# A gated cross-attention layer on one core: the statistics of pass 1 pinned behind the norms, and two gate projections kept for the passage

## The chip, the core and the metric

The kernel runs on one core of a Trainium2 chip. The core has a matrix engine (PE, TensorE, with PEld as its weight loads), a vector engine (DVE), a scalar engine (ACT), GpSimd (POOL), and SP, which here only issues DMAs. Each engine works through its own queue of instructions in order, and engines wait for one another through semaphores. The metric is the time in microseconds of one execution on the device. Before the change it is 2236.16 us, the median of three runs (2235.13 to 2239.27).

## The reference

All in float32. x is 64 sequences of 128 tokens with 512 features; the context is of the same shape; there are 4 heads of 128. Two residual layers follow one another:

```python
Q, K, V = (per head) LN(x) @ Wh, ctx @ Wh, ctx @ Wh
scores = einsum('bshe,bthe->bhst', Q, K) / sqrt(hd)
masked = scores * Dn[None]
A = maximum(abs(masked.sum(axis=0)), 1.0)     # summed over ALL 64 sequences
O = einsum('hst,bthe->bshe', A, V)
Y = (O - mu) / sqrt(var + 0.001) * gn_gamma + gn_beta
W = relu(LN(x) @ wg_w)
x = x + tanh(g_xattn) * ((W * Y) @ wo_w)
# then, on the new x:
g = (LN(x) @ gate_w.T) * gate_s;  u = (LN(x) @ up_w.T) * up_s
x = x + tanh(g_ffn) * (((silu(g) * u) @ down_w.T) * down_s)
```

The sum over the batch axis is what shapes the kernel: A needs the scores of every sequence before the first output token can be made. So there is a pass over all of x for the scores, and a second pass for everything that uses A.

## The kernel before

**Tiling.** The 64 sequences are 16 groups (NG) of 4 (GB), a group being 512 tokens. A group's x lies in two tiles `x_t` (pool `xin`, five buffers). Large matrix products are done by a seven-product scheme on 2x2 blocks; one `product` (L288) is four matmuls of 128x256, and the trace counts two records for each of them.

**Pass 1** (the loop over g at L592 and after) has, per turn, three generators that `interleave` mixes by their number of steps:
- `prepare(g)`: the statistics of group g on DVE (`bn_stats` L252, `bn_aggr` L253 four times, then `ve` L247) and a power on POOL (L248) that gives `rstd`; then, four times, a norm on DVE (`xn` L280, noted in `last_norm`), four transposes on PE (`pt` L259) and a copy of the result into `xnT` (odd ones on DVE, L514, even ones on ACT, L516).
- `scores(g-1)`: `pq` (L524) from `xnT`, its copy `qw` on ACT, `sv` (L539) with the context tiles, its copy `both` on ACT (L547), a store of the values to DRAM (`v_scr`, L549) by SP, and the running sum `attn` on DVE (L555).
- `project(g-1)`: the gate projection, seven steps of one `product` each (L567 to L588) over four DVE sums `t` (L325), with additions on DVE (`w`, L579 and L582) and copies on ACT; the result is stored to `w_scr`.

The two FFN matrices are rewritten for the seven-product scheme during pass 1 as well: `prepare_weights`, one step per turn, loads a block (SP), sums it on POOL (L325 to L336, L439) and stores it (SP). The parts are wo, five blocks of gate and up weights (`gu_raw`), and three of down weights (`dn_raw`, with ten further sums in a tile `dn_t` that has one buffer). The step's instructions are issued after the turn's x load has been.

**The order on an engine** is decided at build time by a planner which places instructions by its own estimate of when they can start; what the program says with `tc.issue_after(ins)` holds an instruction behind `ins` on its engine. Before, only the statistics of group 1 are held so, behind the last norm of group 0. In the order as built, DVE has the statistics of a group two turns ahead of its norms.

**The passage.** In the last turn (g = 15) the projection of group 14 is given 3 of its 7 steps; what is left of it, and all of the projection of group 15, form `tail`. After the last `sv`, attn is multiplied by the decay, and its absolute value and maximum are taken (L625 to L628). Then two strings spell out the order by hand: T is one step of `tail`, R one of `retention(0)` (`po` L653, its statistics, the transposes `pt` L683, the gated product `w_t`), A one of `attended(0)` (`bx`, `by`, `bz` L731: the output projection, whose weights `wo_w` SP loads, L728; then the norm for the FFN and its transposes), P one of the first four of `retention(1)`.

**Pass 2** runs the FFN of group g (`ffn`: gate and up products at L288, the sums `h` at L336, down products at L1009), interleaved with the rest of the attention of later groups. For g = 0 these are the remaining steps of retention 1, `attended(1)` by way of `late_attended`, and retention 2. In `retention`, WAIT (8) empty steps stand between the loads that turn o into `yT` and the use of it (`yT` scaled on ACT, L703; `w_t` on POOL and DVE, L712); for group 1 there are 3 more. `n_steps` tells `interleave` how many steps the second chain has.

Of the kernel before, what the change touches and what calls it, by code (L numbers as in the profile page):

```python
# [99 lines left out]
def interleave(*weighted):  # L100

    runs = [[gen, steps, 0] for gen, steps in weighted if gen is not None]
    while runs:
        run = min(runs, key=lambda r: (r[2] + 1) / r[1])
        try:
            next(run[0])
            run[2] += 1
        except StopIteration:
            runs.remove(run)


def in_order(steps, **gens):

    for name in steps:
        next(gens[name], None)
    for gen in gens.values():
        for _ in gen:
            pass
# [8 lines left out]
def flamingo_gated_layer(  # L127
# [22 lines left out]
    P = 128  # L150
# [6 lines left out]
    NG = B // GB  # L157
# [36 lines left out]
    def load_ctx(g):  # L194
        tiles = []
        for j in range(GB):
            t = cin.tile([P, H, S], F32, tag="c", name="c_t")
            nc.sync.dma_start(out=t, in_=ctxT[g * GB + j])
            tiles.append(t)
        return tiles  # L200
# [175 lines left out]
    def gate_weights():  # L376

        combine_a(
            nc.gpsimd, [wgc[:, m] for m in (GS1, GS2, GS3, GS4)],
            wgc[:, GA11], wgc[:, GA12], wgc[:, 7], wgc[:, GA22],  # L380
        )
# [116 lines left out]
    def prepare(g, x_t, xnT):  # L498

        n = GB if g else 1  # L500
        for j in range(GB):
            bn(mean_var[:, g * GB + j, :], x_t[j // 2][:, j % 2, :])
            if (j + 1) % n == 0:
                cols = slice(g * GB + j + 1 - n, g * GB + j + 1)
                inv_std(rstd[:, cols], mean_var[:, cols, 1], LN_EPS, n)
        yield
        for j in range(GB):
            b = g * GB + j
            xn = normalised(
                x_t[j // 2][:, j % 2, :], mean_var[:, b, 0:1], rstd[:, b : b + 1]  # L510
            )
            pt = transposed(xn, "pt")
            if j % 2:
                nc.vector.tensor_copy(xnT[:, :, j * S : (j + 1) * S], pt)  # L514
            else:
                nc.scalar.copy(xnT[:, :, j * S : (j + 1) * S], pt)  # L516
            yield
# [73 lines left out]
    pending = None  # L591
    weights = prepare_weights()  # L592
    for g in range(NG):
        x_t, c_t = x_next.pop(0), c_next
        xnT = wide.tile([P, NC, TOK], F32, tag="xT", name="xnT")
        prep = prepare(g, x_t, xnT)
        if g == 1:
            with tc.issue_after(last_norm[0].ins):
                next(prep)
        else:  # L600
            next(prep)
        if g == 1:
            gate_weights()
            constants()
        elif g > 1:
            with tc.issue_after(last_load[0].ins):
                next(weights, None)
        held = project(pending[0], pending[2]) if pending else None

        steps = 3 if g == NG - 1 else 7  # L610
        interleave(
            (prep, GB),
            (scores(*pending) if pending else None, 2 + H),
            (islice(held, steps) if pending else None, steps),
        )
        x_next.append(load_x((g + 2) % NG))
        if g + 1 < NG:
            c_next = load_ctx(g + 1)
        pending = (g, c_t, xnT)
# [26 lines left out]
    def retention(g, v, ws):  # L646

        helper = nc.vector if g < 3 else nc.gpsimd

        o = att.tile([P, GB, H, P], F32, tag="yT", name="o")  # L650
        for h in range(H):
            po = ps_mm.tile([P, GB, P], F32, tag="mm", name="po")
            nc.tensor.matmul(  # L653
                po, lhsT=attn[:, h, :], rhs=v[:, h, :, :], start=True, stop=True
            )
            if g < 2 and h % 2:
                nc.vector.tensor_copy(o[:, :, h, :], po)
            else:
                nc.scalar.copy(o[:, :, h, :], po)
            yield  # L660
        if g:
            sq = att.tile([P, NQ, NC, GB, SQ], F32, tag="sq", name="sq")
        ons = []
        for j in range(GB):
            oj = o[:, j].rearrange("p h e -> p (h e)")
            mv = stat.tile([P, 2], F32, tag="mv", name="mv")
            bn(mv, oj)
            rs = stat.tile([P, 1], F32, tag="rs", name="rs")
            inv_std(rs, mv[:, 1:2], GN_EPS, 1)
            if g:  # L670
                square_transposed(sq, j, normalised(oj, mv[:, 0:1], rs))
            else:
                nc.vector.tensor_scalar(oj, oj, mv[:, 0:1], rs, ALU.subtract, ALU.mult)
                ons.append(oj)
        if g == 0:
            for q in range(2):
                tok = slice(q * HT, (q + 1) * HT)
                for d in range(2):
                    pt = ps_mm.tile([P, KC, HT], F32, tag="mm", name="pt")
                    for c in range(KC):  # L680
                        e = (d * KC + c) * P
                        for i in range(2):
                            nc.tensor.transpose(  # L683
                                pt[:, c, i * P : (i + 1) * P], ons[2 * q + i][:, e : e + P], ident
                            )
                    y = att.tile([P, KC, HT], F32, tag="xn", name="y", bufs=2)
                    for c in range(KC):
                        e = d * KC + c
                        nc.scalar.activation(
                            y[:, c, :], pt[:, c, :], AF.Identity,  # L690
                            scale=gamma_sb[:, e : e + 1], bias=beta_sb[:, e : e + 1],
                        )
                    (helper if d else nc.gpsimd).tensor_tensor(
                        ws[q][:, d], ws[q][:, d], y, ALU.mult
                    )
                    yield
            return
        yT = att.tile([P, NQ, NC, GB, SQ], F32, tag="yT", name="yT")
        moved(yT, sq, sq_scr[0][g % 2])
        for _ in range(WAIT + 3 * (g == 1)):  # L700
            yield
        for e in range(NC):
            nc.scalar.activation(  # L703
                yT[:, :, e], yT[:, :, e], AF.Identity,
                scale=gamma_sb[:, e : e + 1], bias=beta_sb[:, e : e + 1],
            )
        yield
        for d in range(2):
            for q in range(2):
                for k in range(KC):  # L710
                    w = ws[q][:, d, k, :].rearrange("p (g i b) -> p i g b", i=NQ, b=SQ)
                    (helper if d else nc.gpsimd).tensor_tensor(  # L712
                        w, w, yT[:, :, d * KC + k, q * 2 : q * 2 + 2, :], ALU.mult
                    )
            yield
# [82 lines left out]
    WAIT = 8  # L798
    RET_STEPS = 4 + WAIT + 2
    ATT_STEPS = 8 + GB  # L800

    def new_x1nT():
        return wide.tile([P, NQ, NC, GB, SQ], F32, tag="xT", name="x1nT")

    ws = None
# [10 lines left out]
    x_t = x_next.pop(0)  # L816
    first, second = next_retention(0), next_retention(1)
    x1nT = new_x1nT()
    tail = chain(held, project(pending[0], pending[2]))
    for name in "TTRRRRTTTRTRTRTRR":  # L820
        next(tail if name == "T" else first, None)
    in_order("ATATATAAAAAPAPAPAPA", A=attended(0, x_t, ws, x1nT), T=tail, P=islice(second, 4))
    pass1.close()

    AHEAD = 9
# [229 lines left out]
    gu_next = [gate_up(0)]  # L1055
    FFN_STEPS = 2 + 7 * NJ + 3 + (len(DOWN_STEPS) - DOWN_ROOTS + 1) // 2
    def late_attended(g, x_t, x1nT):
        yield from attended(g, x_t, ws, x1nT)

    pending = (0, x_t, x1nT, combine_tokens(nc.vector, x1nT))  # L1060
    for g in range(NG - 1):
        x_t = x_next.pop(0)
        x1nT = new_x1nT()
        if g + 2 < NG:
            x_next.append(load_x(g + 2))
        steps = [attended(g + 1, x_t, ws, x1nT)] if g else [second]
        n_steps = ATT_STEPS + RET_STEPS
        if g == 0:
            steps.append(late_attended(1, x_t, x1nT))
            n_steps += RET_STEPS - 4 + 3  # L1070
        if g + 2 < NG:
            steps.append(next_retention(g + 2))
        interleave(
            (ffn(*pending), FFN_STEPS), (chain(*steps), int(n_steps * 1.4)),
        )
        with tc.issue_after(mid_down[0].ins):
            tokens = combine_tokens(nc.vector, x1nT)
        pending = (g + 1, x_t, x1nT, tokens)
# [59 lines left out]
```

## Time and profile before

| | us |
|---|---|
| median of three runs (range) | 2236.16 (2235.13 to 2239.27) |
| the profiled execution: its own time | 2241.91 |
| the profiled execution: its span | 2240.1 |
| PE busy | 2214.0 (99%) |
| DVE busy | 1171.2 (52%) |
| POOL busy | 666.2 (30%) |
| ACT busy | 640.7 (29%) |
| last `sv` of pass 1 ends, about | 390.4 |
| first product of pass 2 (`bank_a` L891) | 433.95 |

The profile is one execution. Its span is what the engines show from the first to the last instruction; the execution's own time is a little longer. "Busy" is the time in which an engine has an instruction at work, "idle before" the time an engine stood still just ahead of one, with the instruction or DMA that released it. In rows of a timeline, the first number is the start in microseconds from the span's start, the second the duration of the row, `x8` the number of like instructions in it, and the bracket the idle time before. The waits are sums over the span or over a stretch of it: total, count, longest. In a table of windows each engine has its busy time and number of instructions, and the three numbers at the end are the granted clock of PE (1.00 is full speed), the share of time of the DMA engines, and GB/s.

### The profile page before, as it was taken

To read this page: it belongs to the slowest core of one execution; us is meant where nothing else is said; L and a number is where in the kernel's file an instruction comes from. 1 tells how busy PE (TensorE), PEld (TensorE's weight loads), DVE (VectorE), ACT (ScalarE), POOL (GpSimd) and SP (SyncE) were. 2 spreads that over 40 slices of the span, in tenths; PEclk is the share of its full clock that TensorE was granted. 3 is DMA by queue.
4 is the path that set the end of the run, shared out by engine and by line. 5 is a ranking of instruction groups with operands and counts; after the bars stand their busy time and mean duration, and the time that the engine had idled before them with its cause. 6 is when DMAs were issued, how large, how long until landed. Compare 5 with 4: busy or idle time off the path is not lost.

```text
span 2240.1 us, 28797 instructions
## 1 busy us (share of the span) xinstructions
PE 2214.0 (99%) x10112; PEld 1889.5 (84%) x10112; DVE 1171.2 (52%) x2827; ACT 640.7 (29%) x1240; POOL 666.2 (30%) x1047
## 2 busy tenths in 40 slices
PE   8999999999999999999999999999999999999999
PEld 7777788778888888888888888888888888888888
DVE  6445443656464636464646464646464646464524
ACT  3444445322222222222222222222222313131221
POOL 4126300241333333333333332323232424141220
PEclk9999999999999999999999999999999999999999
DMA  9778665667877787777777777777777777766654
GB/s 307 261 271 303 240 231 197 253 221 260 276 255 262 249 267 248 265 247 258 251 263 248 253 255 261 249 266 245 266 244 267 244 271 240 277 214 239 226 181 146
DMA packets 216865, 558.47 MB, mean 249 GB/s; under 512 B 21265, under 2 KB 62993, under 8 KB 199953
## 3 DMA queue, kind: packets, MB, share of 16 engines
q1 hardware_dynamic: 211296, 539.58, 71.8%
q10 hardware_dynamic: 5424, 17.04, 2.0%
q8 instruction: 81, 1.33, 0.2%
q14 instruction: 64, 0.52, 0.1%
HBM read 454.31 MB, written 102.24 MB: 248 GB/s over the span
## 4 chain that ended last, share of the span: by engine, by line
PE 93%; DMA 3%; DVE 2%; POOL 1%; SPq 1%; issue 0%; ACT 0%; ACTq 0%; POOLq 0%; DVEq 0%
PE bank_c L288 21%; PE bank_a L288 14%; PE bank_c L1009 9%; PE bank_f L288 7%; PE bank_b L288 7%; PE bank_b L1009 6%; PE sv L539 4%; PE bank_f L1009 4%; PE bank_a L1009 4%; PE by L731 3%; PE bz L731 2%; PE bx L731 2%; PE po L653 2%; PE pq L524 2%; PE bank_c L891 2%; DMA x_t<-in_x_dram 2%
## 5 line engine op out<-in xcount | busy, mean ns | idle before, releaser
L288 PE MATMUL bank_c<-tcomb,gu 128*128 128x256 f32 x1920 | 454.9, 380 | 1.0 <-DVE c L968 0.7
L288 PEld LDWEIGHTS bank_c<-tcomb,gu 128*128 128x128 f32 x1920 | 363.3, 190 | 59.6 <-issue 6.7
L336 POOL TENSOR_TENSOR h<-h 128x128 f32<-128x128 f32 x576 | 258.6, 481 | 399.3 <-DVE h L881 286.1
L288 PE MATMUL bank_a<-x1nT,gu 128*128 128x256 f32 x1280 | 303.7, 379 | 1.6 <-ACT sil L906 1.6
L288 PEld LDWEIGHTS bank_a<-x1nT,gu 128*128 128x128 f32 x1280 | 242.7, 190 | 47.9 <-issue 13.4
L1009 PE MATMUL bank_c<-dn_w,h 128*128 128x256 f32 x896 | 211.7, 379 | 0.0
L1009 PEld LDWEIGHTS bank_c<-dn_w,h 128*128 128x128 f32 x896 | 170.2, 190 | 23.1
L880 ACT ACTIVATE sil<-c,gs_sb 128x256 f32<-128x256 f32 x176 | 89.3, 508 | 328.9 <-DVE c L968 170.7
L248 POOL TENSOR_TENSOR rs<-ve,mhalf 128x1 f32<-128x1 f32 x128 | 73.5, 586 | 321.7 <-DVE ve L247 221.5
L712 POOL TENSOR_TENSOR w_t<-w_t,yT 128x256 f32<-128x256 f32 x112 | 91.5, 848 | 243.3 <-ACT yT L703 243.3
L742 POOL TENSOR_TENSOR x_t<-x_t,m 128x512 f32<-128x512 f32 x48 | 62.1, 1323 | 341.9 <-ACT m L752 341.9
L968 DVE TENSOR_TENSOR c<-bank_c,m 128x512 f32<-128x512 f32 x80 | 55.3, 691 | 202.4 <-PE bank_c L288 201.0
L1009 PE MATMUL bank_b<-dn_w,h 128*128 128x256 f32 x640 | 156.4, 379 | 0.0
L336 DVE TENSOR_TENSOR h<-h 128x128 f32<-128x128 f32 x608 | 152.5, 308 | 4.3
L288 PE MATMUL bank_f<-tcomb,gu 128*128 128x256 f32 x640 | 151.2, 379 | 0.0
L288 PE MATMUL bank_b<-x1nT,gu 128*128 128x256 f32 x640 | 151.2, 379 | 0.0
L288 PEld LDWEIGHTS bank_b<-x1nT,gu 128*128 128x128 f32 x640 | 121.6, 190 | 22.1 <-issue 6.2
L252 DVE BATCH_NORM_STATS2 st<-x_t 128x6 f32<-128x512 f32 x128 | 83.8, 681 | 103.5 <-DMA x_t<-in_x_dram 102.3
L1009 PEld LDWEIGHTS bank_b<-dn_w,h 128*128 128x128 f32 x640 | 121.6, 190 | 16.5
L288 PEld LDWEIGHTS bank_f<-tcomb,gu 128*128 128x128 f32 x640 | 121.6, 190 | 16.5
L1029 DVE TENSOR_TENSOR x_t<-x_t,bank_c 128x256 f32<-128x256 f32 x192 | 77.6, 419 | 87.7 <-PE bank_c L1009 87.7
L539 PE MATMUL sv<-qw,c_t 128*128 128x256 f32 x512 | 120.5, 379 | 1.8 <-DVE xnT L514 1.8
(152 smaller groups left out, 3292.2 us busy)
## 6 DMA issues: line engine op xcount, KB each, us to landing
dn_w<-dn_scr SPq DMA_DIRECT2D x320, 384.0 KB, 4.9
gu<-gu_scr SPq DMA_DIRECT2D x80, 1024.0 KB, 7.8
gu<-gu_scr SPq DMA_DIRECT2D x80, 768.0 KB, 6.1
x_t<-in_x_dram SPq DMA_DIRECT2D x62, 512.0 KB, 5.4
sq_scr<-sq SPq DMA_DIRECT2D x30, 1024.0 KB, 4.7
wo_w<-wo_scr SPq DMA_DIRECT2D x112, 256.0 KB, 3.9
dn_w<-dn_scr SPq DMA_DIRECT2D x96, 256.0 KB, 5.0
c_t<-in_ctxT_dram SPq DMA_DIRECT2D x64, 256.0 KB, 5.2
```

Source lines behind the costliest of these rows:

```text
L248: nc.gpsimd.tensor_tensor(dst, ve, mhalf[:, :n], ALU.pow)
L252: nc.vector.bn_stats(st, src)
L288: last_product[0] = nc.tensor.matmul(out, lhsT=w[:, s, k, :], rhs=x_k, start=(start and s == 0 and k == 0), stop=(s == 1 and k == KC - 1), ...
L336: engine.tensor_tensor(slots[to], slots[a], slots[b], ALU.add if sign == "+" else ALU.subtract)
L539: nc.tensor.matmul(sv[:, 0 : 2 + i : 1 + i, :], lhsT=c_t[j][:, h, :], rhs=qw[:, h, j : GB + 1 : GB - j, :], start=(i == 0), stop=(i == 1), ...
L712: (helper if d else nc.gpsimd).tensor_tensor(w, w, yT[:, :, d * KC + k, q * 2 : q * 2 + 2, :], ALU.mult)
L731: nc.tensor.matmul(bank[:, i * HN : (i + 1) * HN], lhsT=lhs[:, k, i * P : (i + 1) * P], rhs=w[:, k, :], start=(start and i == 0 and k == 0 ...
L742: engine.tensor_tensor(dst, dst, src.rearrange("p (b d) -> p b d", b=2), ALU.add)
L880: nc.scalar.activation(sil, gate, AF.Silu, scale=gs_sb[:, i : i + 1])
L968: nc.vector.tensor_add(c22, bank_c, m5)
L1009: last_down[0] = nc.tensor.matmul(places[acc], lhsT=hq[q][:, a, :], rhs=dn[n][:, q, :], start=start, stop=True, skip_group_check=True,)
L1029: add = nc.vector.tensor_tensor(dst, dst, places[acc], ALU.add if sign > 0 else ALU.subtract)
```

## The change

Five places are edited. The statistics of every group but the first are now held behind the last norm of the group before it. In the last turn no step of the projection of group 14 is made (`project(14)` isn't begun there), so all 14 steps of the last two projections are in `tail`, and the two strings have three T more between them. Retention 1 has 8 empty steps, as all others, and `attended(1)` begins with four.

```diff
-        if g == 1:
+        if g:
+
             with tc.issue_after(last_norm[0].ins):
                 next(prep)
         else:
...
-        steps = 3 if g == NG - 1 else 7
+        steps = 0 if g == NG - 1 else 7
         interleave(
             (prep, GB),
             (scores(*pending) if pending else None, 2 + H),
-            (islice(held, steps) if pending else None, steps),
+            (islice(held, steps) if pending and steps else None, steps),
         )
...
-        for _ in range(WAIT + 3 * (g == 1)):
+        for _ in range(WAIT):
             yield
...
-    for name in "TTRRRRTTTRTRTRTRR":
+    for name in "TTTRRRRTTTTRTRTRTRR":
         next(tail if name == "T" else first, None)
-    in_order("ATATATAAAAAPAPAPAPA", A=attended(0, x_t, ws, x1nT), T=tail, P=islice(second, 4))
+    in_order("AATATATATAAAPAPAPAPA", A=attended(0, x_t, ws, x1nT), T=tail, P=islice(second, 4))
...
     def late_attended(g, x_t, x1nT):
+        for _ in range(4):
+            yield
         yield from attended(g, x_t, ws, x1nT)
...
-            n_steps += RET_STEPS - 4 + 3
+            n_steps += RET_STEPS - 4 + 4
```

## The prediction

> **What bounds the kernel now.** I read the page's busy shares first, then the waits of PE, then PE's own rows for every gap over 0.1 us, and then the queues of the engines that the gaps name. The busy shares say almost everything about the size of the stakes:
>
> ```profile
> PE 2214.0 (99%) x10112; PEld 1889.5 (84%) x10112; DVE 1171.2 (52%) x2827; ACT 640.7 (29%) x1240; POOL 666.2 (30%) x1047
> ```
>
> PE is busy 2214.0 of the span's 2240.1 us. Its gaps add up to 22.95 us; 6.5 lie in the first 20 us, which the change leaves alone; from 550 us on there is none. So a change of order can win at most 7.9 us in pass 1 (gaps at 85.45, 139.05, 164.22, 189.63, 193.44, 268.25 and 277.08: 1.51, 0.72, 0.95, 1.39, 0.27, 1.23, 1.83) and some 9.5 us in the passage and the first group behind it. PE's list of waits names their causes:
>
> ```profile
> PE pq L524 <- DVE xnT L514: 3.1, 3, 1.4
> PE bx L731 <- POOL w_t L712: 2.5, 2, 1.5
> PE sv L539 <- DVE xnT L514: 1.8, 1, 1.8
> PE by L731 <- DVE st L252: 1.5, 1, 1.5
> PE bank_c L288 <- DVE w L579: 1.5, 1, 1.5
> ```
>
> Each number is the total, the count and the longest. The DVE copies are late because DVE works in order and stands in front of them, waiting for x. The list of waits for the first 400 us shows it (first row), beside POOL, which mostly waits for DVE's `ve`:
>
> ```profile
> POOL rstd L248 <- DVE ve L247: 154.9, 17, 23.8
> DVE st L252 <- DMA x_t<-in_x_dram: 102.3, 25, 8.2
> ```
>
> One instance from DVE's rows: the first bn_stats of a group two ahead waits 6.44 us for its tile, and the norms and copies of the nearer group come behind it.
>
> ```profile
> 255.57 0.69 DVE L252 BATCH_NORM_STATS2 st<-x_t 128x6 f32<-128x512 f32 x1 [6.44 <-DMA x_t<-in_x_dram]
> ...
> 258.98 0.97 DVE L280 TENSOR_SCALAR xn<-x_t,mean_var,rstd 128x512 f32<-128x512 f32 x1
> 259.87 0.68 DVE L582 TENSOR_TENSOR w<-bank_b,m5p 128x512 f32<-128x512 f32 x1
> 260.47 0.67 DVE L514 COPY xnT<-pt 128x512 f32<-128x512 f32 x1
> ```
>
> **Part 1, the pin.** Call the four norms of group g n0 to n3, its statistics (four bn_stats, four aggregates, one `ve`) S(g), the POOL power r(g). Before, DVE ran S two groups ahead of the norms; the built order of the changed kernel puts S(g+1) directly behind n3(g). Nothing is added or removed: 64 bn_stats move. What goes: the 102.3 us of DVE waits for x, since x of group g+1 landed a group earlier. What comes: S and r now stand in the chain from n3(g) to n0(g+1): four bn_stats at 0.6, aggregates and `ve` about 0.9, the power 1.0: some 4.3, 4.9 with hand-offs. Before, n0(g+1) came 5.8 to 12.7 us after n3(g), so DVE alone would be in time.
>
> POOL works in order too. Its weight sums now come between. Per group I put the built order of POOL on the times of its rows: r(2) to r(7) end before their norms are due; r(8) at 185.4 for a copy needed by 189.45; r(9) at 210 with 3.7 us to spare; r(12) to r(15) are safe. r(11) isn't: before, it ran at 222.79, ahead of the last block of down weights; now it stands behind that block's ten dn_t sums, six scalings and seven further sums. POOL's rows of before for that block:
>
> ```profile
> 247.63 1.01 POOL L248 TENSOR_TENSOR rstd<-ve,mhalf 128x4 f32<-128x4 f32 x1 [23.83 <-DVE ve L247]
> 252.39 5.72 POOL L336 TENSOR_TENSOR dn_t<-dn_raw 128x256 f32<-128x256 f32 x8 [3.75 <-DMA dn_scr<-dn_t]
> 258.06 0.92 POOL L336 TENSOR_TENSOR dn_t<-dn_t,dn_raw 128x256 f32<-128x256 f32 x1
> ...
> 259.62 1.60 POOL L439 TENSOR_TENSOR dn_raw<-dn_raw,minus_ds 128x256 f32<-128x256 f32 x2
> ...
> 265.01 6.86 POOL L336 TENSOR_TENSOR dn_raw<-dn_raw 128x256 f32<-128x256 f32 x8
> ```
>
> The sums can't start before 252.39, when the store of the block before has left dn_t. Ten sums, six scalings and seven sums at 0.72 (the 5.72 of eight) are 16.5 us, the power 1.0: about 269.9; at the rows' rate later on, 0.86 (6.86 of eight), it is 272; 269.1 at 0.68. DVE then owes n0(11) 0.54, w of L582 0.69 and the copy behind them 0.68, so the copy ends at 271.0 to 273.9. PE needs that copy for this:
>
> ```profile
> 264.20 1.88 PE L524 MATMUL pq<-xnT,gram 128*128 128x512 f32 x4
> ```
>
> A stall of 6.8 to 9.7 us takes the place of 7.9 us of gaps (the 1.23 and 1.83 just behind it among them). I take 7.5, near the low end, as DVE stands still then and leaves POOL the 0.72. The granted clock is a further term. After the two idles of 1.05 and 1.47 us at 472 to 476, it fell to half:
>
> ```profile
> 476.00:478.00 2.00, 2.00 (x5) 1.64 (x6) 1.34 (x2) 0.00 (x0) 2.00 (x4) 0.50 0.00 0
> ```
>
> Three matmuls there took 2.7 us and not 1.3, so a longer idle costs 1.4 to 1.7 more; single gaps up to 1.83 left it at 1.00. I take 1.5. Pass 1: -7.9 + 7.5 + 1.5 = +1.1; the ends are -7.9 + 6.8 + 1.4 = +0.3 and -7.9 + 9.7 + 1.7 + 0.8 (a late ACT copy behind it, two thirds of the 1.23) = +4.3.
>
> [...]
>
> **Part 2, products kept for the passage.** Last group: 10 of PE's matmuls (4.32 us at 0.432) move from before the last `sv` to behind it. Their work is unchanged, so only cover counts. Let E be the end of the last sv (390.42 before). PE has 12 matmuls, 5.18 us, and then `po`, which needs v. The load of v was issued at 391.64 and landed at 397.43, E + 7.0, hidden by 8.2 us of products; now E + 5.2 leaves 1.85 idle. One product waits for `t` behind the norms, 0.8 to 1.1. Against that, the gaps 0.40, 0.47 and 0.14 before the pt transposes go, and 1.51 at `by`, which in truth waits for a wo_w load (issued 421.84, landed 426.64) that now goes out ahead of w_t's. The 0.56 and 1.60 (an ACT table load) stay: +1.85 + 0.95 - 1.01 - 1.51 is +0.3; my step-by-step sum of the new order gives +0.4. The bounds are +/- 2.0: nothing idle at v and t below, both at full and by's wait kept above. SP issues the same loads as before in another order; one that goes out late is in these bounds.
>
> **Part 3, the wait of retention 1 and the four extra yields.** PE's first `bx` of group 1 waits for POOL's w_t. POOL, before:
>
> ```profile
> 469.10 3.56 POOL L336 TENSOR_TENSOR h<-h 128x128 f32<-128x128 f32 x8 [6.77 <-DVE h L881]
> 472.61 1.41 POOL L712 TENSOR_TENSOR w_t<-w_t,yT 128x256 f32<-128x256 f32 x2
> ```
>
> Built before, 16 h sums of the FFN stand ahead of that w_t; built now, 27. Eleven more at 0.44 (3.56 / 8) are 4.9 us; at 0.70 in the busiest rows, 7.7. The wait is for the same instructions, only later: w_t ends some 5 us on, while PE got one product's 1.3 us more of cover. So +4.9 - 1.3 = +3.6; PE's second wait at 475.99 shrinks by 0.2: +3.4. Ends: +1.0, if the h are ready enough earlier for POOL to fill its 6.77 us of idleness, to +6.0 (7.7 - 1.3 - 0.4). The half clock is there in both kernels. Later groups keep their order and cover.
>
> **Sum.** 1.1 + 0.4 + 3.4 = +4.9. The profiled execution took 2241.91 (span 2240.1 and 1.8 around it), 5.75 over the median of 2236.16; I add the difference to the median: 2241.1. Own range 2236 (0.3 - 1.6 + 1.0 = -0.3) to 2249 (4.3 + 2.4 + 6.0 = 12.7). A measurement of this kernel tells 0.2%, 4.5 us, from no change: under 2231.7 is faster, over 2240.6 slower.
>
> **Rivals.**
> - *The cover on POOL holds* (faster). If r(11) ends by 262.3 (264.20 less 0.54, 0.69, 0.68), PE never waits there and all 7.9 us of pass 1 are won; that needs dn_t free at 245.5, seven us earlier than its store landed. For it: DVE's earlier work may draw PE, and with it SP's store issue at 238.76, forward by the 4.8 us of gaps that lie before. Against: PE's need comes forward as much. With +0.4 and attended(1) at +1: 2229.7. Chance 0.24.
> - *Given back exactly.* Stall at 6.8, v lands before PE asks (-1.6), POOL fills its idleness (+1.0): 0.3 - 1.6 + 1.0, so 2235.9. For it: the terms are of one size and opposed. Chance 0.14.
> - *POOL slower than its rows*: at 0.91 a sum, as in its rows at 194 and 202, r(11) ends past 273 and r(8), with 2 us to spare, is late too; every term at its upper end gives 2248.9. Against: with DVE stalled, POOL is alone. Chance 0.16.
> - *My forecast*, 0.46, of which 0.14 ends under 2240.6.
>
> Faster 0.24, same 0.14 + 0.14 = 0.28, slower 0.32 + 0.16 = 0.48. The range from 2229 to 2249 leaves out about 2 in 10.
>
> **What would show it.** In the changed profile: DVE's waits at L252 for x_t near nothing; POOL's rstd of group 11 near 269 and a PE gap of about 7 us at a pq L524 some 260 us in, released by the xnT copy or the norm, with clock under 1.00 behind it; a PE gap of 1 to 2 us at the first po; bx waiting on w_t for 4 us or more near 475 and none at by. The forecast is wrong if that pq has no gap (faster), or if w_t comes no later than before.

## The result, and the profile after

The changed kernel takes 2242.99 us (median of 13 runs, 2241.48 to 2244.47) against 2236.82 for the kernel before (13 runs beside it): a ratio of 1.0025, 95% interval 1.0017 to 1.0032. It is slower, by some 6 us where 4.9 were forecast. The profiled execution of after took 2244.25, with a span of 2242.5. The page's first lines hide the change entirely:

```profile
PE 2216.7 (99%) x10112; PEld 1893.9 (84%) x10112; DVE 1180.3 (53%) x2827; ACT 642.5 (29%) x1240; POOL 663.4 (30%) x1047
```

PE is "busy" 2.7 us more for the same 10112 instructions: the work is the same and parts of it took longer, at the lower clock that the windows below show. PE's list of waits tells more (total, count, longest):

```profile
PE pq L524 <- DVE xnT L514: 6.8, 1, 6.8
...
PE bx L732 <- POOL w_t L713: 4.3, 1, 4.3
...
PE po L654 <- DMA v<-v_scr: 0.8, 1, 0.8
```

The many small waits of pass 1 are gone; one wait of 6.8 us is left, beside 4.3 us at bx (2.5 before). DVE's own waits show that the pin did what it says: for x it waits 5.7 us in all, where it waited 102.3.

```profile
DVE st L252 <- DMA x_t<-in_x_dram: 5.7, 3, 3.8
```

**The wait of 6.8 us.** It is read backwards, engine by engine. PE's rows:

```profile
258.43 1.89 PE L288 MATMUL bank_a<-xnT,wgc 128*128 128x256 f32 x8
267.11 3.78 PE L524 MATMUL pq<-xnT,gram 128*128 128x512 f32 x4 [6.79 <-DVE xnT L514]
270.68 1.06 PE L259 MATMUL pt<-ident,xn 128*128 128x128 f32 x4
```

DVE, whose copy PE waits for, itself stood still for 13.38 us in front of the first norm of group 11; the copy is two instructions behind that norm and doesn't depend on it:

```profile
247.85 0.70 DVE L247 TENSOR_SCALAR ve<-mean_var 128x4 f32<-128x4 f32 x1
...
264.92 0.94 DVE L280 TENSOR_SCALAR xn<-x_t,mean_var,rstd 128x512 f32<-128x512 f32 x1 [13.38 <-POOL rstd L248]
265.78 0.68 DVE L582 TENSOR_TENSOR w<-bank_b,m5p 128x512 f32<-128x512 f32 x1
266.38 0.68 DVE L514 COPY xnT<-pt 128x512 f32<-128x512 f32 x1
```

And POOL, which had what it needed for that rstd (`ve` ends at 248.55), did 23 sums and scalings first:

```profile
247.80 5.89 POOL L336 TENSOR_TENSOR dn_t<-dn_raw 128x256 f32<-128x256 f32 x8 [22.87 <-DMA dn_scr<-dn_t]
...
259.12 4.80 POOL L336 TENSOR_TENSOR dn_raw<-dn_raw 128x256 f32<-128x256 f32 x7
263.88 1.00 POOL L248 TENSOR_TENSOR rstd<-ve,mhalf 128x4 f32<-128x4 f32 x1
```

POOL had stood idle for 22.87 us just before. The power wasn't ready then; it became ready 0.75 us after the sums began, and its own result came 16.3 us after that.

**The price behind the wait.** The four `pq` records behind the stall take 3.78 us, and 1.88 in the kernel before. The windows of two microseconds show why (the number after the five engines is the granted clock):

```profile
262.00:264.00 2.00, 0.00 (x0) 0.00 (x0) 0.00 (x0) 0.00 (x0) 2.00 (x4) 0.69 1.10 341
264.00:266.00 2.00, 0.00 (x0) 0.00 (x0) 1.08 (x2) 0.00 (x0) 1.57 (x2) 0.50 0.99 301
...
270.00:272.00 2.00, 2.00 (x8) 1.29 (x7) 1.33 (x3) 1.26 (x3) 0.00 (x0) 0.50 1.02 397
272.00:274.00 2.00, 2.00 (x9) 1.69 (x8) 0.33 (x1) 0.36 (x1) 0.00 (x0) 0.75 1.06 400
```

A window's mean clock of 0.69 means that 1.24 of its 2 us were at half: the clock fell at about 262.8 and came back at about 273.0. PE resumed at 267.1 and so worked 5.9 us at half speed, a loss of some 2.9 us on top of the 6.8.

**bx of group 1.** POOL's rows again show a short operation behind many sums:

```profile
469.69 8.07 POOL L336 TENSOR_TENSOR h<-h 128x128 f32<-128x128 f32 x19 [6.76 <-DVE h L882]
477.72 1.40 POOL L713 TENSOR_TENSOR w_t<-w_t,yT 128x256 f32<-128x256 f32 x2
```

**What the two given profiles don't agree on.** The spans differ by 2.4 us (2240.1 and 2242.5), the medians by 6.2. The profiled execution of before took 2241.91, 5 us over its median, so its gaps might not be those of a usual execution. That was the first thing to test.

### The profile page after: what moved, and what is told of

It is laid out like the page before. It is cut to its first block, busy times and chain, and to the rows that moved or that the text cites. A ratio compares the mean times of both kernels' runs of the same rounds, so it can differ in the third digit from the quotient of the medians.

```text
span 2242.5 us, 28798 instructions
## 1 busy us (share of the span) xinstructions
PE 2216.7 (99%) x10112; PEld 1893.9 (84%) x10112; DVE 1180.3 (53%) x2827; ACT 642.5 (29%) x1240; POOL 663.4 (30%) x1047
## 4 chain that ended last, share of the span: by engine, by line
PE 95%; DMA 2%; POOL 1%; DVE 1%; issue 0%; ACT 0%; SPq 0%; ACTq 0%; POOLq 0%; DVEq 0%
PE bank_c L288 22%; PE bank_a L288 14%; PE bank_c L1010 9%; PE bank_b L288 7%; PE bank_f L288 7%; PE bank_b L1010 6%; PE sv L539 5%; PE bank_f L1010 4%; PE bank_a L1010 4%; PE by L732 3%; PE bx L732 3%; PE bz L732 2%; PE po L654 2%; PE pq L524 2%; PE bank_c L892 2%; PE pt L259 1%
## 5 line engine op out<-in xcount | busy, mean ns | idle before, releaser
L248 POOL TENSOR_TENSOR rs<-ve,mhalf 128x1 f32<-128x1 f32 x128 | 73.3, 585 | 287.4 <-DVE ve L247 264.6
L901 ACT COPY bank_c<-bank_a 128x256 f32<-128x256 f32 x16 | 5.7, 357 | 401.8 <-PE bank_a L892 401.8
```

The source lines that it names most:

```text
L248: nc.gpsimd.tensor_tensor(dst, ve, mhalf[:, :n], ALU.pow)
```

## The experiments

Times are medians beside the kernel before on the same chip (before took 2236.30 to 2236.82 in the four sets of runs, so two medians of different sets compare to about half a microsecond); "gaps" are PE's idle times over 0.1 us from its rows.

**The kernel before, profiled again** (no edit).

> The kernel before, unchanged, for a second profile of it. The two profiles so far differ by 2.35 us of span (2240.1 before, 2242.5 after), the medians by 6.2; the profiled execution of before took 2241.91, 5 us over its median. Theory A, that the traced execution of before had wider gaps than most: PE's gaps in pass 1 add up to 2 to 5 us here instead of 7.9, and the time is 2234 to 2238. Theory B, that the gaps are the same in every execution: 7.9 us again within 1 us, and what differs lies elsewhere (the start, the clock).

2240.12 us in this one execution, span 2238.3. PE's waits, of which the pq and sv lines for `xnT` are those of pass 1:

```profile
PE pq L524 <- DVE mean_var L253: 3.6, 1, 3.6
...
PE sv L539 <- DVE xnT L514: 2.2, 1, 2.2
PE pq L524 <- DVE xnT L514: 1.9, 3, 1.2
```

Behind the first 24 us the gaps of pass 1 come to 4.51 us, not 7.90: theory A for the gaps. The expected time was missed: this execution lost 3.6 us at one wait in its first 20 us (0.9 in the given profile), so the start varies too. In the run of the passage alone, whose pass 1 is ordered as before, the gaps are 2.69. So these gaps are draws. In the given profile the chain that ended last has a load of x ahead of most of them, so the landing of the x tiles is the likely cause; the 1.51 at 85.45 of the given profile has no counterpart in the other two.

**The pin alone, and everything but the pin.**

```diff
 (before, pin_only)
-        if g == 1:
+        if g:
             with tc.issue_after(last_norm[0].ins):
 (after, passage_only)
-        if g:
+        if g == 1:
             with tc.issue_after(last_norm[0].ins):
```

> Only the pin of the statistics; projections, strings and waits as before. Theory A (the pin wins the gaps of pass 1 and loses them at the rstd of group 11, whose stall and half clock cost 9.7 us by the two profiles): within -1 and +6 us of before, 2236 to 2243, with a PE gap of about 6.8 us at a pq some 260 us in. Theory B (the pin is a gain, and the passage and attended(1) cost it): 5 us or more faster than before.

> All of the change but the pin. Theory A: the profiles give -1.7 for the passage and +1.75 for attended(1), so no change, 2235 to 2239; pass 1 has the gaps of before, and bx waits 4 us for w_t. Theory B: +4 us or more.

Pin alone: 2239.90 us against 2236.30, ratio 1.0013 (1.0004 to 1.0022), with the same stall:

```profile
PE pq L524 <- DVE xnT L514: 6.9, 1, 6.9
```

All but the pin: 2238.14, ratio 1.0008 (0.9999 to 1.0016), with bx waiting 4.29 us. So the larger part of the loss lies in pass 1, the smaller (+1.8, whose interval just reaches no change) in the rest, and 3.6 + 1.8 make 5.4 of the 6.2. Theory A holds; that the pin as it stands is a gain is out.

**Group 11 not pinned.**

```diff
 (after, pin_not_11)
-        if g:
+        if g and g != 11:
             with tc.issue_after(last_norm[0].ins):
```

> The changed kernel with the statistics of group 11 alone not pinned, so that their power stands on POOL ahead of the ten dn_t sums again. Theory A: the stall of 6.8 us and its half clock (2.9) go, some 1 to 2 us of waits for x come back: 7 to 9 us under the changed kernel, 2234 to 2236, so 0.05 to 0.15% faster than before. Rival: the stall only moves to group 12 or 13 or to the next sum on POOL: within 3 us of the changed kernel.

2233.04 us, ratio 0.9980 (0.9971 to 0.9989): 10 us under the changed kernel, a little more than the 7 to 9 expected. One condition on one of 16 groups turns the loss into a gain. The power of group 11 now runs 20 us ahead of the sums, as in these POOL rows, and PE's only gap of pass 1 is 1.11 us:

```profile
226.96 1.01 POOL L248 TENSOR_TENSOR rstd<-ve,mhalf 128x4 f32<-128x4 f32 x1 [2.04 <-DVE ve L247]
246.80 6.14 POOL L336 TENSOR_TENSOR dn_t<-dn_raw 128x256 f32<-128x256 f32 x8 [18.84 <-DMA dn_scr<-dn_t]
```

**The powers ahead of the weight sums, all groups pinned.**

```diff
 (after, powers_first)
...
-        nc.gpsimd.tensor_tensor(dst, ve, mhalf[:, :n], ALU.pow)
+        last_power[0] = nc.gpsimd.tensor_tensor(dst, ve, mhalf[:, :n], ALU.pow)
...
-            with tc.issue_after(last_load[0].ins):
+            with tc.issue_after(last_load[0].ins), tc.issue_after(last_power[0].ins):
                 next(weights, None)
```

> The changed kernel with each turn's weight sums on POOL held behind that turn's power, so every rstd stands ahead of the sums and all groups stay pinned. Theory: what the pin costs is only the place of one power behind 23 sums, so the 6.8 us stall and its half clock go: 8 to 11 us under the changed kernel, 2232 to 2235, no PE gap over 1 us between 25 and 385 us. Rival: the sums, now waiting for powers, store their weights later and PE stalls elsewhere, or the first products of the FFN wait for gu: less than 5 us under the changed kernel.

2233.52, ratio 0.9987 (0.9979 to 0.9996), and no PE gap between 25 us and the end of pass 1. The two ways of getting the power out early agree within 0.5 us, so it is the power's place on POOL that costs, not the group or the pin.

**w_t ahead of the h sums.** A hold on the FFN's first POOL sums, alone and with the powers first:

```diff
 (after, gate_first; powers_first, both_first)
...
-                    (helper if d else nc.gpsimd).tensor_tensor(
+                    ins = (helper if d else nc.gpsimd).tensor_tensor(
                         w, w, yT[:, :, d * KC + k, q * 2 : q * 2 + 2, :], ALU.mult
                     )
+                    if d == 0 and g == 1:
+                        last_gate[0] = ins
...
                 for e, q, one in todo[:part]:
-                    sum_tiles(e, h_slots[q], (one,))
+                    if g == 0 and e is nc.gpsimd:
+                        with tc.issue_after(last_gate[0].ins):
+                            sum_tiles(e, h_slots[q], (one,))
+                    else:
+                        sum_tiles(e, h_slots[q], (one,))
```

> The changed kernel with the FFN's first h sums on POOL held behind the four w_t of retention 1. Theory: 19 h sums (8.07 us in the trace) are what bx waits for; then w_t waits only for ACT's yT (the first two end near 473.2 in the changed trace), the gap of 4.27 at bx shrinks to about 1 us and most of the half clock behind it goes: 2 to 5 us under the changed kernel, 2238 to 2241. Rival: yT, or the x_t sums that come after the h sums, take the place of the wait: within 1 us of the changed kernel.

> Both edits together: the powers ahead of the weight sums and w_t ahead of the h sums. If the two costs are independent the gains add: 10 to 15 us under the changed kernel, 2228 to 2233, faster than before by 0.15 to 0.4%. Rival, that one stall hides the other's: no better than the better of the two by more than 1 us.

Both missed. Alone: 2245.04, ratio 1.0036 (1.0024 to 1.0049); with the powers: 2235.63, 0.9993 (0.9985 to 1.0002), where powers alone had 0.9987. The gap at bx is gone, and the time isn't. POOL's rows of the first of the two:

```profile
470.31 2.79 POOL L713 TENSOR_TENSOR w_t<-w_t,yT 128x256 f32<-128x256 f32 x4 [23.83 <-ACT yT L704]
473.07 12.64 POOL L336 TENSOR_TENSOR h<-h 128x128 f32<-128x128 f32 x24
485.68 3.70 POOL L745 TENSOR_TENSOR x_t<-x_t,m 128x512 f32<-128x512 f32 x3
```

w_t comes at 470.31, but the additions to x_t now stand behind 24 sums. PE, same run:

```profile
477.97 3.33 PE L734 MATMUL bz<-wo_w,ys 128*128 128x256 f32 x8 [2.10 <-DVE ys L328]
...
488.93 3.56 PE L734 MATMUL bz<-wo_w,ys 128*128 128x256 f32 x8 [3.82 <-DVE x_t L745]
```

First DVE's `ys` is late (2.10), then x_t (3.82), and each is followed by a slow product (3.33 and 3.56 us instead of 1.89). The rival had the mechanism: the wait only moved. It also grew (5.92 us where 4.27 went), and past the rival's bound of 1 us.

**The h sums behind x_t as well**, the hold being on the last of POOL's three x_t additions.

```diff
 (both_first, x_first)
...
-            engine.tensor_tensor(dst, dst, src.rearrange("p (b d) -> p b d", b=2), ALU.add)
+            return engine.tensor_tensor(dst, dst, src.rearrange("p (b d) -> p b d", b=2), ALU.add)
...
         for q, d in ((0, d2), (1, d2), (1, d1)):
-            add(nc.gpsimd, q, d, m1)
+            ins = add(nc.gpsimd, q, d, m1)
+        if g == 1:
+            last_gate[0] = ins
```

> Powers first and w_t first as in the run with both, and the h sums held behind POOL's three x_t additions of attended(1) as well. There bz waited 2.10 us for DVE's ys and 3.82 for x_t, which stood behind 24 h sums. Theory: the 3.82 and its half clock go, the 2.10 stays: 4 to 6 us under that run (2235.6), 2229.5 to 2232. Rival: a wait for the h sums themselves or for another x_t addition takes its place: within 2 us of 2235.6.

2233.73, ratio 0.9985 (0.9976 to 0.9994): 1.9 us better than the run without, not 4 to 6. The wait for x_t (3.83 in that run) went, the one for ys stayed (2.08 there, 2.42 here), and a new gap of 2.01 appeared 20 us later, at a gate product that waits for DVE's `c`. The rival by its number, and much the same as leaving the h sums alone (2233.52).

**The waits of retention 1 put back.**

```diff
 (after, wait_back)
-        for _ in range(WAIT):
+        for _ in range(WAIT + 3 * (g == 1)):
...
     def late_attended(g, x_t, x1nT):
-        for _ in range(4):
-            yield
...
-            n_steps += RET_STEPS - 4 + 4
+            n_steps += RET_STEPS - 4 + 3
```

> The changed kernel with the three empty steps of retention 1 put back and the four of attended(1) taken out. In the order as built the 27 h sums stand ahead of w_t all the same, and bx at the same place, so theory: 2242 to 2244, bx waits 4.3 us; the lateness of w_t comes from the projections kept for the passage and not from the waits. Rival: as the prediction had it, the waits set it: 2 us or more under the changed kernel.

2242.22, ratio 1.0024 (1.0015 to 1.0034), as the changed kernel, and bx waits as long:

```profile
PE bx L732 <- POOL w_t L713: 4.3, 1, 4.3
```

The third part of the change is worth nothing that can be measured. By elimination, w_t's late place comes with the projections kept for the passage; by what step of the planner is not shown.

**The pin and the powers on the kernel before**, with its passage left as it was, and the same with w_t and x_t of group 1 ahead of the h sums. The edits are those above.

> The kernel before with the pin of all groups and the powers ahead of the weight sums; projections, strings and waits as before. Theory: the projections kept for the passage cost 1.8 us (the run of that part alone) and nothing in the passage itself, so this is 1 to 3 us under the changed kernel with powers first (2233.5), 2230.5 to 2232.5, 4 to 6 us under before. Rival: with pass 1 free of stalls the kept projections win back what they cost: 2233 or more.

> The run above with w_t and x_t of group 1 ahead of the h sums too. Before had gaps of 1.05 and 1.47 at bx and a half clock behind them. Theory: these go and DVE's ys comes in as a wait of at most 2 us: 0 to 3 us under the run above, 2228 to 2232. Rival: DVE's ys costs more than the two gaps: 1 us or more over it.

The first: 2232.60, ratio 0.9982 (0.9973 to 0.9991), the lowest median of the study (the run with group 11 not pinned, 2233.04, is within the scatter of it): 0.9 us under the changed kernel with powers first, against 2236.46 for before. The expected 1 to 3 us are just missed, and 0.9 us alone is within the scatter, so that the kept projections cost something in this setting rests on the stage times below. POOL's rows show how the hold works. The power goes first, and the block behind it, in another order of its parts, starts at 247.83, where it started at 247.80 in the changed kernel:

```profile
246.86 1.01 POOL L249 TENSOR_TENSOR rstd<-ve,mhalf 128x4 f32<-128x4 f32 x1 [22.97 <-DVE ve L248]
247.83 1.59 POOL L440 TENSOR_TENSOR dn_raw<-dn_raw,minus_ds 128x256 f32<-128x256 f32 x2
...
253.70 6.97 POOL L337 TENSOR_TENSOR dn_raw<-dn_raw 128x256 f32<-128x256 f32 x8
260.64 6.60 POOL L337 TENSOR_TENSOR dn_t<-dn_raw 128x256 f32<-128x256 f32 x8
```

The second: 2237.53, 1.0005 (0.9997 to 1.0014), 5 us worse, its rival. The two gaps at bx shrink from 1.05 and 1.47 to 0.41 and 0.24, and then DVE, POOL and PE in turn (one view each):

```profile
470.70 12.88 POOL L337 TENSOR_TENSOR h<-h 128x128 f32<-128x128 f32 x29
483.55 1.16 POOL L249 TENSOR_TENSOR rs<-ve,mhalf 128x1 f32<-128x1 f32 x2
```

```profile
484.13 1.16 DVE L281 TENSOR_SCALAR xn<-x_t,mv,rs 128x512 f32<-128x512 f32 x2 [5.54 <-POOL rs L249]
...
490.41 0.68 DVE L975 TENSOR_TENSOR c<-bank_c,m 128x512 f32<-128x512 f32 x1
```

```profile
491.15 3.38 PE L289 MATMUL bank_c<-tcomb,gu 128*128 128x256 f32 x8 [5.35 <-DVE c L975]
```

This is the stall of pass 1 in another place: a power (`rs`) behind a block of sums on POOL, a norm waiting for it on DVE, and behind the norm the instruction that PE needs.

**The stages side by side**, from PE's rows. Pass 1 is from the first transpose of group 1 to the end of the last sv; 4.32 us of kept products are added to it, and taken from the passage, where they were moved. The passage ends at the first product of the FFN, and the last column runs on to its first down product. Everything behind it takes 1714.6 to 1715.0 us in all of them.

| kernel | pass 1 (gaps in it) | passage | FFN 0 to its down products |
|---|---|---|---|
| before, given profile | 370.5 (7.9) | 43.4 | 88.4 |
| before, again | 367.0 (4.5) | 41.9 | 87.9 |
| all but the pin | 364.7 (2.7) | 41.8 | 89.7 |
| pin alone | 370.0 (6.9) | 41.8 | 87.9 |
| after | 370.7 (6.8) | 41.6 | 90.2 |
| waits put back | 369.3 (5.2) | 41.6 | 89.8 |
| group 11 not pinned | 362.2 (1.1) | 41.8 | 89.3 |
| powers first | 360.8 (0) | 41.9 | 89.8 |
| pin and powers, passage as before | 360.8 (0) | 41.8 | 87.9 |
| w_t first | 370.3 (6.7) | 41.8 | 91.8 |
| w_t and powers first | 360.8 (0) | 41.9 | 91.8 |
| w_t, x_t and powers first | 360.8 (0) | 42.0 | 88.6 |
| pin and powers, w_t and x_t first, passage as before | 360.8 (0) | 41.9 | 92.2 |

Each row is one execution. That of w_t, x_t and powers first lies 1.5 us under its median.

## Why the prediction was right, point by point

The direction, the place and the chain were right, and the time lies 1.9 us over the forecast. That it lies so near is in part luck: terms of the sum were off both ways by up to 2.5 us. By its steps:

- **The pin removes DVE's waits for x.** Right: 102.3 us fell to 5.7, and with the powers first pass 1 has no gap left.
- **r(11) is late on POOL and PE stalls at a pq.** Right in place, and in size at the low end: 6.79 us, where 6.8 to 9.7 were given and 7.5 taken; the three other executions with the stall have 6.89, 6.68 and 5.19. The times themselves were not met: the sums began at 247.80 and not at 252.39, the power ended at 264.88 and not near 269, and PE asked at 260.32 and not at 264.20. The first rival asked whether the store that frees dn_t would come forward with the gaps that go, and the argument against it was that PE's need would come forward too: both did, by 4.6 and 3.9 us, so the stall stayed. The sums took the lower price: 0.74 us (5.89 for eight) while DVE was busy 2.87 of the 5.89 us, 0.69 (4.80 for seven) while it stood still, as argued; in the run of the pin and the powers, with DVE at work (5.50 of 6.90 us), eight of them took 6.97. That the power's place is the cause is shown by undoing it in two ways, 9.5 to 10 us each.
- **The clock behind the stall**, 1.5 taken: too small. The 1.7 of the upper end is what the 3.4 us at half in the given profile of before come to (475.8 to 479.2). At the stall PE worked 5.9 us at half speed, 2.9 lost; in the run of the pin alone 4.2 us, 2.1 lost (by the stages, 370.0 - 360.8 - 6.9 is 2.3).
- **The 7.9 us that go**: too large as a price for the median. Pass 1 without gaps takes 360.8, and the three executions in the order of before 364.7, 367.0 and 370.5. The pin is worth 4 to 10 us, 6.6 in the mean, and the stall with its clock takes 9.2 (the pin alone) to 9.9 (the changed kernel) back. Pass 1 alone measures +3.6 by the median of the pin alone (+2.6 by its stages) where +1.1 was forecast. This is the term that was off most; its bound, +4.3, held.
- **The passage**, +0.4: measured -0.2 (41.6 against 41.9 in the second profile of before). po waited 0.77 and not 1.85: v's load was issued at 388.67, 0.25 us after the last sv, where it had been 1.2, and landed after 5.7. The saving of 1.51 at `by` wasn't one, since the second profile of before has no such gap.
- **attended(1)**, +3.4: measured +1.4 to +2.3 (89.3 to 90.2 against 87.9). w_t came at 477.72, where 477.5 was forecast. The mis-sized part is what followed: the second wait of bx (1.47) vanished with the first, as all four w_t were then done, and the gap of 0.67 further on too. And the half clock, taken as alike in both kernels, wasn't: behind bx PE worked 6.1 us at half in the changed kernel, 3.2 in the given profile of before, and none in the second one behind the same two gaps. The first of these rows is of the changed kernel, the second of before, profiled again:

```profile
480.00:482.00 2.00, 2.00 (x6) 1.46 (x5) 1.06 (x3) 0.75 (x2) 0.90 (x2) 0.50 0.00 0
```

```profile
474.00:476.00 2.00, 1.31 (x6) 1.19 (x7) 0.65 (x1) 0.00 (x0) 2.00 (x4) 1.00 0.00 0
```

- **Part 3 as the cause of w_t's lateness**: wrong. Put back, the waits change nothing; it belongs to part 2.

Three errors partly cancel, +2.5 in pass 1 against -0.6 and -1.6, and leave 0.3 of difference by this account; the median moved by 6.2, so about 1 us is left, which single profiles can't place. A slip without weight: the gaps of the passage and the first group behind it add up to 8.5 us and not "some 9.5"; no term uses it.

## What to carry to other kernels

When an instruction is pinned on one engine, follow what depends on it into the other in-order queues: a power of 1 us behind 23 ready sums and scalings cost 9.5 to 10 us, and holding the sums behind the power gave it all back. Order by who is waited for, not by who is ready; but bringing one item forward only helps if what it pushes back has slack, as the four runs with the h sums show. The gaps of pass 1 came to 7.9, 4.5 and 2.7 us in three profiles of one order: price such gaps from several profiles, not from one.

## What the runs showed of the hardware that was not expected

The half clock lasted about 3.4 us at 476 in the given profile of before (475.8 to 479.2, from the windows' mean clocks), 6.8 at bx in after (477.8 to 484.6) and 10.2 at the stall in after (262.8 to 273.0). In the run of the pin alone an equal stall, 6.89 against 6.79 us, had 6.8 us of it, from 264.6 to 271.4, which began 4.3 us into the stall and not 2.4:

```profile
264.00:266.00 2.00, 0.00 (x0) 0.00 (x0) 0.96 (x2) 0.00 (x0) 1.70 (x3) 0.65 1.01 308
...
270.00:272.00 2.00, 2.00 (x9) 1.33 (x8) 1.49 (x4) 1.42 (x4) 0.00 (x0) 0.65 1.02 398
```

So two stalls of nearly one length lost 2.1 and 2.9 us to the clock. PE resumed at 267.1 in the changed kernel, 5.9 us before the clock came back at 273.0, and at 267.2 with the pin alone, 4.2 us before it came back at 271.4. Shorter idle times differ as well: behind the gaps of 1.05 and 1.47 us at bx the clock was at half for 3.4 us in the given profile of before, and in the second profile it stayed at 1.00 behind the same two. What makes the clock fall and come back when it does isn't shown by these runs; for a stall of 6.8 or 6.9 us these two profiles give a price of clock of 2.1 to 2.9 us, and not one number.
